# One core, eight blocks: the opening's loads, biases and masks are reordered, and three batches' expert rows are turned by VectorE and DMA

## The chip, the core and the metric

The kernel runs on one core of a Trainium2 chip. TensorE (PE) multiplies matrices, VectorE (DVE), ScalarE (ACT) and GpSimd (POOL) work on tiles, and SyncE (SP) starts transfers; ScalarE and GpSimd can start transfers too. The metric is the device time of one launch in microseconds (us).

## The reference

Four layers run over `x` (4 batches, 256 tokens, 256 features). Each adds a cross-attention over a context (4 batches, 512 rows of 128) and then a feed-forward block, both on the layer-normed `x`:

```python
...
    x = x + _L0_xattn_ref(_layernorm(x, axis=-1), ctx_1024, L0_xattn_Wq, ...)
    x = x + _L0_ffn_ref(_layernorm(x, axis=-1), L0_ffn_A, L0_ffn_B, L0_ffn_W, L0_ffn_bias)
    x = x + _L1_xattn_ref(_layernorm(x, axis=-1), ctx_1024, mask_BxS2_bf1, L1_xattn_Wq, ...)
...
```

Layer 0's attention has 16 heads of 16 lanes; queries and keys get a bias and are normed by head, and the last 16 rows of the context go through weights of their own (`Wkv_dca`, `bkv_dca`). Layer 0's feed-forward block takes, of 64 small experts (16 rows of A each), the four with the largest response to a token and adds their outputs to a dense product. The other layers' attention has 16 heads of 128; their blocks are gated experts, two experts by argmax, and a top-64 selection of tokens. Only layer 0 is touched by the change.

## The kernel before

`bounded_path` (L837) is the program that runs. In each engine's queue the order of the work is the order in which the Python code calls it, since the section is a hand-ordered schedule (L1055); transfers go to the queue of the engine that is named.

**The opening** (L1059 to L1596). SP loads x of batch 0 and the query weights `wq0`, then three short bias rows into `rows1` (its part `crow`: q's bias, the keys' bias, the bias of the special keys), then the second context, the second x, and the rest. ScalarE's queue loads the first context (`load_c(0)`, L872) and the weights `wkv` for keys and values. GpSimd loads the norms' parameters `prm`. A load uses one of eight transfer semaphores in turn, so with eight under way the next one waits for an earlier one.

TensorE begins with `warm(9)` (L1464): multiplications of the identity by itself, which have no use but to keep the engine busy. `context_T(0)` (L907) turns the four 128x128 blocks of the first context (pcT), and ScalarE copies them to `cT`. `Norm` (L915) takes mean and variance on DVE and the inverse root on GpSimd; `tokens` writes the normed rows; `layernorm_T` (L939) turns them by four TensorE blocks (pxn) and one copy by ScalarE. `centred` (L1178) takes each head's mean out of the weights and of the bias rows, on DVE. `rows_of_biases` (L1120) makes three rows of zeros and ones (`takes`), on GpSimd, that say which bias row a partition gets; `spread_biases` (L1188) multiplies them with `crow` (pbias), and ScalarE copies the result to `bqk`. `project_q` (L1207) multiplies queries (pq) and gives back the addition of the bias (DVE, L1219); `project_k` (L1223) does it for the keys (pk, L1235). Then squares, sums, powers and scales (class `Scale`) lead to the turned heads (pT) and to the first scores (ps L1401) at 20.96 us.

**Layer 0's attention** (L1707 to L1724). For each batch b and each of eight steps i (four groups of heads, two halves of the keys) the queues get, in this order: the scores of the step (16 products, in four of the six PSUM banks of one ring) and their exponentials on ScalarE (L1405); `ahead`; the products with the values of the group before (po); at odd steps `quotient` (L1428, DVE); and `between(b, i)` (L1613), which spreads the other work over the steps: the next batch's projections, norms and turned heads, the output of the batch before (`output0`), and at the end the beginning of the expert block.

`turned_aside` and `layernorm_aside` (L969) are another way to turn a tile: DVE turns blocks of 32x32 into `y`, and 16 transfers on SP's queue put the blocks in place. The contexts of batches 2 and 3 go this way.

**The expert block** (class `Arrows`, L1471; loop at L1749). Eight chunks of 128 tokens. `vectors` multiplies by `wa` (paf), `routes` picks four experts on DVE and ends with a product on GpSimd (L1514), `turned` turns that by TensorE (puT), `output` adds up (pyf). The normed rows `xnTs["f", k]` of batch k are turned by `layernorm_T`: batch 0 and 1 at steps 3 and 5 of the last batch's attention (L1698), 2 and 3 in the loop (L1767).

Of the kernel before, what the change touches and what calls it, by code (L numbers as in the profile page):

```python
# [836 lines left out]
def bounded_path(ctx: ExitStack, tc: tile.TileContext, t, out: bass.AP, over):  # L837
# [34 lines left out]
    def load_c(b):  # L872
        (nc.sync if b else nc.scalar).dma_start(c_sb[:, b], t["ctx"][b].rearrange("(k p) c -> p k c", p=P))
# [181 lines left out]
    with tc.manual_schedule(engines={E.PE, E.Activation, E.DVE, E.Pool}):  # L1055
# [4 lines left out]
        load_c(0)  # L1060
# [3 lines left out]
        wkv = l0.tile([P, 2, 2 * D], F32, tag="wkv", name="wkv")  # L1064
        nc.scalar.dma_start(wkv[:, 0, :], t["L0_wkv"])
# [5 lines left out]
        def by_head(w, x=HD0):  # L1071
            return w.rearrange("p n (h x) -> p n h x", x=x)


        rows1 = w0.tile([3, D + 3 * P], F32, tag="oT0", name="rows1")
        crow = rows1[:, :D].rearrange("n (o d) -> n o d", o=1)
        takes = rows1[:, D:].rearrange("n (i p) -> n i p", p=P)


        brow = l0.tile([1, 2, 2 * D], F32, tag="brow", name="brow")  # L1080
        nc.sync.dma_start(crow[0:1, 0, :], t["L0_bq"].partition_broadcast(1))
        for i, n in enumerate(("L0_bkv", "L0_bdca")):
            nc.sync.dma_start(
                crow[1 + i : 2 + i, 0, :].rearrange("o (h x) -> o h x", x=HD0),
                t[n].rearrange("(o h x) -> o h x", o=1, x=2 * HD0)[:, :, :HD0],
            )
# [101 lines left out]
        def spread_biases():  # L1188
            pb = bank("mm", [P, 2, D], "pbias0")
            for i in range(2):  # L1190
                nc.tensor.matmul(pb[:, i, :], lhsT=takes[:, i, :], rhs=crow[:, 0, :], start=True, stop=True)
            pl = bank("mm", [P, D], "pbias1")
            nc.tensor.matmul(pl, lhsT=takes[:, 2, :], rhs=crow[:, 0, :], start=True, stop=True)
            nc.scalar.copy(bqk[:, 0:2, :], pb)
            nc.scalar.copy(bqk[:, 2, :], pl)
# [111 lines left out]
        def columns_of_norms():  # L1307
            wide = [P, 3, 2, HD0]
            by_lane = l0.tile(wide, F32, tag="by_lane", name="by_lane")
            pairs = l0.tile([P, 3, 2], F32, tag="pairs", name="pairs")  # L1310
            nc.vector.tensor_tensor(by_lane, prm, lane0[:, 0, None, None, :].to_broadcast(wide), ALU.mult)
            nc.vector.tensor_reduce(pairs, by_lane, AX.X, ALU.add)
            for o in range(2):
                nc.vector.tensor_scalar(
                    cols[:, o, :], pairs[:, 0, :], halves0[:, o : o + 1], HD0 ** -0.5, ALU.mult, ALU.mult
                )
            nc.vector.tensor_copy(cols[:, 2:, :], pairs[:, 1:, :])
# [294 lines left out]

        def between(b, i):  # L1613

            n = b + 1
            if n == 1:
# [76 lines left out]
            if b == B - 1:  # L1693
                if i in (0, 2, 6):
                    norms["f", i // 2] = Norm(min(i // 2, 2), f"f0_{min(i // 2, 2)}")
                if i in (1, 3, 7):
                    xns["f", i // 2] = norms["f", i // 2].tokens()
                if i in (3, 5):  # L1698
                    k = (i - 3) // 2
                    xnTs["f", k] = layernorm_T(xns["f", k], f"f0_{k}")  # L1700
                if i == 4:
                    arrows[0] = Arrows(0)
                    arrows[0].vectors()
                if i == 5:
                    arrows[0].routes()
# [43 lines left out]
        for n in range(B * NC):  # L1749
# [1730 lines left out]
```

## Time and profile before

| what | us |
|---|---|
| median of 3 runs | 1381.64 (1380.35 to 1382.58) |
| the profiled execution | 1380.97 |
| its span | 1379.2 |
| first scores of layer 0 (ps L1401) | 20.96 |
| last products of layer 0's attention end | 137.4 |
| first query product of layer 1 (pq L1900) | 220.46 |

The span runs from the first to the last recorded instruction; the rest of the execution's time lies around it. A line of a timeline gives start, length, engine, line of the code, operation, output and inputs with their sizes, and in brackets the idle time before it with what ended it. Lines of the same kind that follow one another are merged (x4). PEld are the loads of TensorE's weights, which run beside its products. A letter q after an engine's name means its queue of transfers. A multiplication in float32 is recorded as two passes, so four products are x8, while turned blocks (pcT, pxn, pT) are recorded once each.

### The profile page before, as it was taken

Reading aid. Unit: us, or ns where it says so; the run is one execution under the profiler, and the core shown is the slowest. Engines: PE = TensorE matmul, PEld = TensorE weight load, DVE = VectorE, ACT = ScalarE, POOL = GpSimd, SP = SyncE. Lnnn points to the kernel's source line nnn. Section 1 sums busy time; section 2 is a strip of 40 time slices with the busy share of each in tenths; the row PEclk is TensorE's granted clock in tenths of the full one; section 3 lists DMA queues with packets and bytes.
Section 4 is the critical chain, followed back from the end, with each engine's and each line's share of the span. In section 5 each row is a group of like instructions: output and inputs, shape, how many; then the busy total and the mean of one; then the engine's idle time right before and its main releaser. Section 6 shows DMA issues by size and latency. Waiting matters only on the chain.

```text
span 1379.2 us, 20227 instructions
## 1 busy us (share of the span) xinstructions
PE 1369.2 (99%) x7221; PEld 903.1 (65%) x7221; DVE 897.2 (65%) x2052; ACT 572.6 (42%) x1134; POOL 699.4 (51%) x848
## 2 busy tenths in 40 slices
PE   9999999999999999999999999999999999999997
PEld 7665676566656667887565666666975665666666
DVE  6767863666666557655676756558656758566675
ACT  5766454433343332256434333333364334333331
POOL 5223333566565445352577655566325676444660
PEclk9999999999999999999999999999999999999999
DMA  5000220300000001361120000000432000000001
GB/s 171 15 3 2 77 78 17 89 19 8 16 5 19 0 13 43 83 218 48 47 54 15 17 0 16 0 1 16 124 119 69 7 12 4 1 8 1 0 1 34
DMA packets 77907, 50.79 MB, mean 37 GB/s; under 512 B 40628, under 2 KB 72645, under 8 KB 77799
## 3 DMA queue, kind: packets, MB, share of 16 engines
q1 hardware_dynamic: 72262, 36.13, 9.6%
q0 software_dynamic: 4176, 12.24, 3.1%
q8 instruction: 59, 0.97, 0.3%
q10 hardware_dynamic: 1360, 1.05, 0.2%
q14 instruction: 50, 0.40, 0.1%
HBM read 38.78 MB, written 6.95 MB: 33 GB/s over the span
## 4 chain that ended last, share of the span: by engine, by line
PE 97%; POOL 2%; DVE 1%; issue 0%; ACT 0%; POOLq 0%; DVEq 0%
PE ps L1948 23%; PE po L1956 23%; PE paq L1918 6%; PE pao L1918 5%; PE pbq L1918 4%; PE pbo L1918 4%; PE ps L1401 3%; PE po L1411 2%; PE pyf L1535 2%; PE paf L1485 2%; PE pgu L2496 2%; PE pm L1014 2%; PE psh L2317 2%; PE py L2042 2%; PE pn L1030 1%; PE pb L2901 1%
## 5 line engine op out<-in xcount | busy, mean ns | idle before, releaser
L1967 POOL TENSOR_TENSOR half<-pT 128x1024 f32<-128x1024 f32 x93 | 218.4, 2349 | 282.8 <-ACT pT L1951 228.0
L1948 PE MATMUL ps<-qT,cT 128*128 128x512 f32 x768 | 345.6, 593 | 0.0
L1956 PE MATMUL po<-pT,c_sb 128*128 128x512 f32 x768 | 345.3, 592 | 0.0
L1951 ACT ACTIVATE pT<-ps,mbias 128x512 f32<-128x512 f32 x384 | 263.8, 687 | 164.0 <-PE ps L1948 147.3
L1956 PEld LDWEIGHTS po<-pT,c_sb 128*128 128x128 f32 x768 | 145.8, 190 | 183.2 <-issue 183.2
L1948 PEld LDWEIGHTS ps<-qT,cT 128*128 128x128 f32 x768 | 138.9, 190 | 138.4 <-issue 136.1
L1960 ACT COPY oT<-po 128x512 f32<-128x512 f32 x96 | 56.2, 586 | 265.2 <-PE po L1956 265.2
L2003 POOL TENSOR_TENSOR oT<-oT,wide 128x512 f32<-128x512 f32 x84 | 106.8, 1291 | 0.0
L1928 DVE TENSOR_TENSOR qT<-qT,paq 128x128 f32<-128x128 f32 x90 | 25.2, 280 | 87.1 <-ACT qT L1927 87.1
L1405 ACT ACTIVATE pT<-ps 128x512 f32<-128x512 f32 x128 | 66.0, 602 | 21.6 <-PE ps L1401 21.4
L1975 DVE TENSOR_TENSOR half<-half 128x512 f32<-128x512 f32 x96 | 71.9, 749 | 2.7 <-POOL half L1965 2.5
L1977 DVE STREAM_TRANSPOSE turned<-half 128x512 f32<-128x512 f32 x96 | 68.3, 711 | 6.3
L1918 PE MATMUL paq<-xnT_a,m_sb 128*128 128x128 f32 x360 | 71.3, 280 | 0.0
L1928 DVE TENSOR_TENSOR w<-w,pao 128x128 f32<-128x128 f32 x21 | 6.0, 285 | 99.2 <-ACT w L1927 99.2
L1918 PE MATMUL paq<-xx,m_x 128*128 128x128 f32 x360 | 69.6, 275 | 0.0
L1918 PEld LDWEIGHTS paq<-xnT_a,m_sb 128*128 128x128 f32 x360 | 57.5, 192 | 18.2 <-issue 9.2
L1981 DVE TENSOR_REDUCE sums<-turned 128x16 f32<-128x512 f32 x96 | 65.9, 686 | 3.3
L1918 PE MATMUL pao<-n_x,ox 128*128 128x128 f32 x336 | 65.0, 275 | 0.0
L1927 ACT COPY qT<-paq 128x128 f32<-128x128 f32 x90 | 23.9, 265 | 94.2 <-PE paq L1918 93.2
L1931 DVE TENSOR_TENSOR qT<-qT,pbq 128x384 f32<-128x384 f32 x90 | 49.8, 554 | 9.4
L1918 PEld LDWEIGHTS paq<-xx,m_x 128*128 128x128 f32 x360 | 54.7, 192 | 0.0
L2002 DVE STREAM_TRANSPOSE wide<-rz 128x512 f32<-128x512 f32 x84 | 54.4, 686 | 0.0
(504 smaller groups left out, 2553.9 us busy)
## 6 DMA issues: line engine op xcount, KB each, us to landing
wq<-in_L_wqT SPq DMA_DIRECT2D x8, 512.0 KB
wo<-in_L_wo SPq DMA_DIRECT2D x8, 512.0 KB
yd<-yr SPq DMA_DIRECT2D x20, 128.0 KB
xnT_a<-y_a SPq DMA_DIRECT2D x144, 16.0 KB
xd<-xn_f SPq DMA_DIRECT2D x8, 256.0 KB
w<-in_F_w SPq DMA_DIRECT2D x4, 512.0 KB
wq<-in_L_wqT POOLq DMA_DIRECT2D x3, 512.0 KB
wo<-in_L_wo POOLq DMA_DIRECT2D x3, 512.0 KB
```

The source lines that it names most:

```text
L1405: nc.scalar.activation(pT[kp][:, j], ps[j], AF.Exp)
L1918: nc.tensor.matmul(p[:, at, :], lhsT=lhsT, rhs=rhs, start=(k == 0 and at == 0), stop=(k == len(of) - 1 and i == which[-1]),)
L1948: nc.tensor.matmul(ps, lhsT=cT[:, b, k * P : (k + 1) * P], rhs=qT, start=True, stop=True)
L1951: nc.scalar.activation(pT[:, k, :], ps, AF.Exp, bias=mbias[:, b, k : k + 1])
L1956: nc.tensor.matmul(po, lhsT=c_sb[:, b, k, :], rhs=pT[:, k], start=(k == 0), stop=(k == NK - 1))
L1960: done["head"] = nc.scalar.copy(raw, po).ins
L1967: nc.gpsimd.tensor_tensor(half, pT[:, 0:2], pT[:, 2:4], ALU.add)
L1975: nc.vector.tensor_tensor(part, half[:, 0], half[:, 1], ALU.add)
L1977: nc.vector.transpose(turned.rearrange("p f i -> p (f i)"), part)
L1981: nc.vector.tensor_reduce(sums[b, hp // 4][:, hp % 4, :], turned, AX.X, ALU.add)
L2002: nc.vector.transpose(wide, rzs[b, hp // 4][:, hp % 4, :, None].to_broadcast([P, NB, 32]))
L2003: eng.tensor_tensor(outs[b, hp], outs[b, hp], wide.rearrange("p f i -> p (f i)"), ALU.mult)
```

## The change

The three bias rows move to the front of ScalarE's queue of transfers, ahead of the first context, which is now called for after `wq0`. The masks `takes` are made by four copies of columns of the identity on DVE instead of memset and selects on GpSimd. `c_last` is zeroed after the first norm. The first context is turned behind the normed rows, the biases are centred ahead of `wq0` and spread ahead of the queries' products, one `warm(3)` before the rows' turning and one before the queries are gone, and the first warm-up has 11 products. In the expert block the rows of batch 0 are normed at step 2 and turned at step 3 of batch 2's attention, those of batch 1 at steps 0 and 1, and those of batch 2 at steps 6 and 7 of batch 3's attention, all three by DVE and 16 transfers each (`rows_of_arrows`) into tiles of their own (`xf`); those of batch 3 stay with TensorE. `kept` in `columns_of_norms` and the pair of calls of `spread_biases` change nothing in the order of what they hold.

```diff
@@ -1057,33 +1057,31 @@
         l0 = c0.enter_context(tc.tile_pool(name="l0", bufs=1, side="right"))
 
         load_x(0)
-        load_c(0)
-        wq0 = l0.tile([P, ND, D], F32, tag="wq0", name="wq0")
-        nc.sync.dma_start(wq0, t["L0_wq"].rearrange("(d p) n -> p d n", p=P))
-
-        wkv = l0.tile([P, 2, 2 * D], F32, tag="wkv", name="wkv")
-        nc.scalar.dma_start(wkv[:, 0, :], t["L0_wkv"])
-        nc.scalar.dma_start(wkv[:, 1, :], t["L0_wdca"])
-
-        prm = l0.tile([P, 3, 2, HD0], F32, tag="prm", name="prm")
-        nc.scalar.preload_act_table_set("natural_log_exp_and_others")
-
-        def by_head(w, x=HD0):
-            return w.rearrange("p n (h x) -> p n h x", x=x)
-
-
         rows1 = w0.tile([3, D + 3 * P], F32, tag="oT0", name="rows1")
         crow = rows1[:, :D].rearrange("n (o d) -> n o d", o=1)
         takes = rows1[:, D:].rearrange("n (i p) -> n i p", p=P)
-
-
-        brow = l0.tile([1, 2, 2 * D], F32, tag="brow", name="brow")
-        nc.sync.dma_start(crow[0:1, 0, :], t["L0_bq"].partition_broadcast(1))
+        nc.scalar.dma_start(crow[0:1, 0, :], t["L0_bq"].partition_broadcast(1))
         for i, n in enumerate(("L0_bkv", "L0_bdca")):
-            nc.sync.dma_start(
+            nc.scalar.dma_start(
                 crow[1 + i : 2 + i, 0, :].rearrange("o (h x) -> o h x", x=HD0),
                 t[n].rearrange("(o h x) -> o h x", o=1, x=2 * HD0)[:, :, :HD0],
             )
+        wq0 = l0.tile([P, ND, D], F32, tag="wq0", name="wq0")
+        nc.sync.dma_start(wq0, t["L0_wq"].rearrange("(d p) n -> p d n", p=P))
+
+        wkv = l0.tile([P, 2, 2 * D], F32, tag="wkv", name="wkv")
+        load_c(0)
+        nc.scalar.dma_start(wkv[:, 0, :], t["L0_wkv"])
+        nc.scalar.dma_start(wkv[:, 1, :], t["L0_wdca"])
+
+        prm = l0.tile([P, 3, 2, HD0], F32, tag="prm", name="prm")
+        nc.scalar.preload_act_table_set("natural_log_exp_and_others")
+
+        def by_head(w, x=HD0):
+            return w.rearrange("p n (h x) -> p n h x", x=x)
+
+
+        brow = l0.tile([1, 2, 2 * D], F32, tag="brow", name="brow")
         load_c(1)
         load_x(1)
         for i, n in enumerate(("L0_bkv", "L0_bdca")):
@@ -1118,17 +1116,11 @@
         pad = l0.tile([P, NQK, 2, P], F32, tag="pad", name="pad")
 
         def rows_of_biases():
-            nc.gpsimd.memset(takes, 1.0)
-            for i, base, cm, p in (
-                (0, 0, -1, 0), (1, -1, 1, 0), (1, 1, -1, 0), (2, RD - 1 - P, P, -1), (2, 2 * P - RD, -P, 1),
-            ):
-                nc.gpsimd.affine_select(
-                    out=takes[:, i, :], in_=takes[:, i, :], compare_op=ALU.is_ge, fill=0.0, base=base,
-                    pattern=[[p, P]], channel_multiplier=cm,
-                )
+            for i, n, h in ((0, 0, slice(0, P)), (1, 1, slice(0, P)), (2, 1, slice(0, RD)), (2, 2, slice(RD, P))):
+                w = takes[:, i, h]
+                nc.vector.tensor_copy(w, ident[:3, n : n + 1].to_broadcast([3, h.stop - h.start]))
 
         c_last = l0.tile([P, 2, 2, P], F32, tag="c_last", name="c_last")
-        nc.gpsimd.memset(c_last, 0.0)
         lane0 = l0.tile([P, 2, HD0], F32, tag="lane0", name="lane0")
         halves0 = l0.tile([P, 2], F32, tag="halves0", name="halves0")
         nc.vector.tensor_reduce(
@@ -1185,14 +1177,11 @@
 
         bqk = l0.tile([P, 3, D], F32, tag="bqk", name="bqk")
 
-        def spread_biases():
-            pb = bank("mm", [P, 2, D], "pbias0")
-            for i in range(2):
-                nc.tensor.matmul(pb[:, i, :], lhsT=takes[:, i, :], rhs=crow[:, 0, :], start=True, stop=True)
-            pl = bank("mm", [P, D], "pbias1")
-            nc.tensor.matmul(pl, lhsT=takes[:, 2, :], rhs=crow[:, 0, :], start=True, stop=True)
-            nc.scalar.copy(bqk[:, 0:2, :], pb)
-            nc.scalar.copy(bqk[:, 2, :], pl)
+        def spread_biases(a, z):
+            pb = bank("mm", [P, z - a, D], f"pbias{a}")
+            for i in range(a, z):
+                nc.tensor.matmul(pb[:, i - a, :], lhsT=takes[:, i, :], rhs=crow[:, 0, :], start=True, stop=True)
+            return lambda: nc.scalar.copy(bqk[:, a:z, :], pb)
 
         qks, xnTs = {}, {}
 
@@ -1310,11 +1299,15 @@
             pairs = l0.tile([P, 3, 2], F32, tag="pairs", name="pairs")
             nc.vector.tensor_tensor(by_lane, prm, lane0[:, 0, None, None, :].to_broadcast(wide), ALU.mult)
             nc.vector.tensor_reduce(pairs, by_lane, AX.X, ALU.add)
-            for o in range(2):
-                nc.vector.tensor_scalar(
-                    cols[:, o, :], pairs[:, 0, :], halves0[:, o : o + 1], HD0 ** -0.5, ALU.mult, ALU.mult
-                )
-            nc.vector.tensor_copy(cols[:, 2:, :], pairs[:, 1:, :])
+
+            def kept():
+                for o in range(2):
+                    nc.vector.tensor_scalar(
+                        cols[:, o, :], pairs[:, 0, :], halves0[:, o : o + 1], HD0 ** -0.5, ALU.mult, ALU.mult
+                    )
+                nc.vector.tensor_copy(cols[:, 2:, :], pairs[:, 1:, :])
+
+            return kept
 
         def score_bound():
 
@@ -1538,28 +1531,27 @@
                 nc.gpsimd.tensor_tensor(x_sb[b][:, c, :], x_sb[b][:, c, :], ys, ALU.add)
 
 
-        warm(9)
-        context_T(0)
+        warm(11)
+        rows_of_biases()
         norm = Norm(0, "a0_0")
-        rows_of_biases()
-        last_context(0)
+        nc.gpsimd.memset(c_last, 0.0)
         mq = head_sums(by_head(wq0))
         xn = norm.tokens()
-        warm(3)
+        centred(by_head(crow), by_head(crow), head_sums(by_head(crow), 3), 3)
         xnTs[0] = layernorm_T(xn, "a0_0")
+        context_T(0)
+        last_context(0)
+        for a, z in ((0, 2), (2, 3)):
+            spread_biases(a, z)()
         centred(by_head(wq0), by_head(wq0), mq)
-        centred(by_head(crow), by_head(crow), head_sums(by_head(crow), 3), 3)
         wk = by_head(wkv, 2 * HD0)[:, :, :, :HD0]
         centred(by_head(wk0), wk, head_sums(wk))
         for n in range(2):
             wv = by_head(wkv, 2 * HD0)[:, n, :, HD0:].rearrange("p (q j o) x -> p o q j x", q=2, o=2)
             for o in range(2):
                 nc.gpsimd.tensor_copy(wvo[:, n, o].rearrange("p (q j) x -> p q j x", q=2), wv[:, o])
-        columns_of_norms()
-        warm(3)
-        add_q = project_q(0)
-        spread_biases()
-        add_q()
+        columns_of_norms()()
+        project_q(0)()
         sc0 = Scale(0)
         sc0.square(True, 0, NC)
         add_k = [project_k(0, k0) for k0 in range(0, NK, 2)]
@@ -1610,9 +1602,18 @@
                 elif i == 7 and n > 1:
                     transposed(n, 4)
 
+        def rows_of_arrows(k):
+            xnT = early.tile([P, ND, S], F32, tag="xf", name=f"xnT_f0_{k}", bufs=3)
+            xnTs["f", k] = layernorm_aside(norms["f"].tokens(), f"f0_{k}", xnT, True)
+
         def between(b, i):
 
             n = b + 1
+            if b == B - 2:
+                if i == 2:
+                    norms["f"] = Norm(0, "f0_0")
+                elif i == 3:
+                    rows_of_arrows(0)
             if n == 1:
                 if i == 0:
                     for k0 in range(0, NK, 2):
@@ -1691,13 +1692,10 @@
                     for j in range(1, 4):
                         nc.vector.tensor_copy(quad[:, 32 * j : 32 * (j + 1)], quad[:, :32])
             if b == B - 1:
-                if i in (0, 2, 6):
-                    norms["f", i // 2] = Norm(min(i // 2, 2), f"f0_{min(i // 2, 2)}")
-                if i in (1, 3, 7):
-                    xns["f", i // 2] = norms["f", i // 2].tokens()
-                if i in (3, 5):
-                    k = (i - 3) // 2
-                    xnTs["f", k] = layernorm_T(xns["f", k], f"f0_{k}")
+                if i in (0, 6):
+                    norms["f"] = Norm(1 + i // 6, f"f0_{1 + i // 6}")
+                if i in (1, 7):
+                    rows_of_arrows(1 + i // 6)
                 if i == 4:
                     arrows[0] = Arrows(0)
                     arrows[0].vectors()
@@ -1762,9 +1760,8 @@
                 if n:
                     arrows[n].output()
             else:
-                k = n // NC + 2
-                if k < B:
-                    xnTs["f", k] = layernorm_T(xns["f", k + (k == 2)], f"f0_{k}")
+                if n == 3:
+                    xnTs["f", 3] = layernorm_T(xns["f", 3], "f0_3")
                 if n == 7:
                     first_xnT = layernorm_T(xn1, "a1_0")
                     next(fold)
```

More of the change, by code (lines that the diff above doesn't have):

```diff
@@ L1059, in bounded_path @@
         load_x(0)
-        load_c(0)
+        rows1 = w0.tile([3, D + 3 * P], F32, tag="oT0", name="rows1")
+        crow = rows1[:, :D].rearrange("n (o d) -> n o d", o=1)
+        takes = rows1[:, D:].rearrange("n (i p) -> n i p", p=P)
+        nc.scalar.dma_start(crow[0:1, 0, :], t["L0_bq"].partition_broadcast(1))
+        for i, n in enumerate(("L0_bkv", "L0_bdca")):
+            nc.scalar.dma_start(
+                crow[1 + i : 2 + i, 0, :].rearrange("o (h x) -> o h x", x=HD0),
+                t[n].rearrange("(o h x) -> o h x", o=1, x=2 * HD0)[:, :, :HD0],
+            )
         wq0 = l0.tile([P, ND, D], F32, tag="wq0", name="wq0")
@@ L1072, in by_head @@
             return w.rearrange("p n (h x) -> p n h x", x=x)
-        rows1 = w0.tile([3, D + 3 * P], F32, tag="oT0", name="rows1")
-        crow = rows1[:, :D].rearrange("n (o d) -> n o d", o=1)
-        takes = rows1[:, D:].rearrange("n (i p) -> n i p", p=P)
         brow = l0.tile([1, 2, 2 * D], F32, tag="brow", name="brow")
-        nc.sync.dma_start(crow[0:1, 0, :], t["L0_bq"].partition_broadcast(1))
-        for i, n in enumerate(("L0_bkv", "L0_bdca")):
-            nc.sync.dma_start(
-                crow[1 + i : 2 + i, 0, :].rearrange("o (h x) -> o h x", x=HD0),
-                t[n].rearrange("(o h x) -> o h x", o=1, x=2 * HD0)[:, :, :HD0],
-            )
         load_c(1)
@@ L1312, in columns_of_norms @@
             nc.vector.tensor_reduce(pairs, by_lane, AX.X, ALU.add)
[L1313 to L1317 removed]
+            def kept():
+                for o in range(2):
+                    nc.vector.tensor_scalar(
+                        cols[:, o, :], pairs[:, 0, :], halves0[:, o : o + 1], HD0 ** -0.5, ALU.mult, ALU.mult
+                    )
+                nc.vector.tensor_copy(cols[:, 2:, :], pairs[:, 1:, :])
+            return kept
         def score_bound():
```

## The prediction

> **What bounds the kernel now.** I read the page first, then the chain of waits for the first 26 us, the timeline of the three places that the change touches (0 to 26, 90 to 138, 138 to 220 us), SP's waits, and the tile views of the turned rows. The page's first part:
>
> ```profile
> PE 1369.2 (99%) x7221; PEld 903.1 (65%) x7221; DVE 897.2 (65%) x2052; ACT 572.6 (42%) x1134; POOL 699.4 (51%) x848
> ```
>
> TensorE is the bound nearly everywhere: work taken off it counts in full, work put on DVE counts only where TensorE then waits. The opening is the exception, since part of its busy TensorE is filler (pwarm). The chain of waits, 0 to 26 us (start, length, what):
>
> ```profile
> 5.74 0.85 PE pcT L911 x4
> 6.59 1.10 PE pwarm L1468 x6
> 7.69 0.44 PE pxn_a L945 x4
> 8.12 0.67 PE pwarm L1468 x6
> 8.79 0.01 issue
> 8.80 1.99 PE pq L1212 x8
> 10.79 1.06 PE pbias L1191 x4
> 11.85 0.43 PE pbias L1193 x2
> 12.28 1.07 PE pk L1229 x4
> 13.36 0.02 issue
> 13.38 0.69 DVE qk L1235
> ```
>
> The reader is to see that TensorE's queue carries the chain up to the first keys (end of pk, 13.36), and that from 13.38 DVE carries it to 17.7. The timeline shows beside it when data come, and SP's waits when the loads land:
>
> ```profile
> 8.71 0.41 DVE L1175 TENSOR_REDUCE hm<-rows 3x16 f32<-3x256 f32 x1 [0.98 <-DMA rows<-in_L_bdca]
> 12.50 0.69 DVE L1219 TENSOR_TENSOR qk<-pq,bqk 128x512 f32<-128x512 f32 x1 [0.56 <-ACT bqk L1194]
> SPq L873 <- DMA wkv<-in_L_wdca: 1.5, 1, 1.5
> SPq L873 <- DMA c_sb<-in_ctx: 1.3, 1, 1.3
> ```
>
> The bias rows arrive at 8.71. The addition of q's bias waits for them until 12.50, but it ends at 13.19, before pk's 13.36: it costs the chain almost nothing.
>
> **The change, part 1: the opening.** Removed from TensorE's path: two warm(3), 1.10 + 0.67 = 1.77 us. Two more warm-ups (4 records of some 0.21, 0.85 in all) fill the place of the four turned blocks of the first context (pcT), so the filler again ends at 6.59. pcT now stands behind pxn. The bias products are only put ahead of pq; TensorE's sum to the end of pk holds them either way. So this reordering removes no time from the chain, only q's wait, which was not last.
>
> New sum: pxn needs the normalised rows (DVE L933, 6.21 + 0.83 = 7.04), so with two blocks before and two after it ends at 7.45. Then pcT 0.44 (pxn's own four blocks, now warm), pbias 1.06 + 0.43, pq 1.99, pk 1.07: 4.99 us. If pcT starts at T, pk ends at T + 4.99, and the gain is 13.36 - 4.99 - T = 8.37 - T. With T = 7.45 that is 0.92 us.
>
> T hangs on the first context's landing. Its issue stood on ScalarE's queue at 0.81 and landed when SP's waiting L873 went on, at 4.75. Now three bias rows stand ahead of it; their issues took 0.37, 0.66 and 0.60 on SP, so it is issued at 2.44. SP, freed of the rows, issues c1 and x1 right behind wq (1.72 and 2.14, not 4.75 and 5.21, as only six to eight loads are out then). So four loads of 256 KB (x0, wq, c1, x1) are issued ahead of the context, where it was second. In the trace the fourth such load, wkv, landed at 6.16 (SP's L1090 goes on) and the fifth, wdca, at 8.20 (L873): bandwidth falls from some 350 to mostly below 60 GB/s between about 6.4 and 7.2 us, while the three rows loaded by POOL are on the same engines. T lies between 7.45 (like wkv) and 8.25 (like wdca); I take 8.17, near the fifth, which it is. Gain 0.2 us, bounds 0.9 and, a further 1 us late, -0.8.
>
> Here a rule speaks against the change. The Trainium skill, "DMA: Bandwidth & Descriptors", section "Issuing engines are not separate DMA queues", says that loads started by different engines run on the same 16 engines and interleave; another queue saves only issue time. The row agrees in part: c_sb and x_sb were issued at 0.81 and 0.80, and the context landed 0.8 us later. With a queue of its own the context would land 3.94 us after its issue as before, at 6.4, and the gain be 0.92; by the rule it is pushed back by c1 and x1, and the gain is 0.2. I follow the rule.
>
> The rest: the four mask copies on DVE (0.16 each by L1317, 0.25 by L1692: 0.6 to 1.0 us) lie in DVE's wait for x (2.31 to 3.92); without it they would cost that. POOL loses its five selects and a memset; c_last's memset (0.56) moves behind rstd and is done before the context is turned. The bias rows' own sums (0.41 + 0.42) now run at 7.04 to 7.87, and put wq's centring from 6.96 to 7.87 to 8.64; pq starts at 10.1, so it is hidden. wkv and wdca are sixth and seventh or later; I estimate 9.5 from the fifth's 8.20 and 0.73 us per load at 350 GB/s. Keys' weights are then ready at 9.5 + 0.67 + 0.78 = 10.95, before pk (12.1); the norms' columns (1.05) end at 12.0, where q's addition wants to start. Another 0.5 us late would be hidden, more counts one for one. ACT's table load (1.28) moves to about 4 and is done before its first copy at 7.5.
>
> Clock: the profile's granted clock reads 1.00 throughout, yet 128x128 blocks take 0.21 each until 7.3 and 0.11 after. The Trainium skill, "TensorE: Matmul & The Clock Gate", Part 1, says half rate lasts until a window of some 3.4 us was busy, and returns after an idle one. The trace took 5.7 us from the first warm-up. By the row nothing changes (TensorE stays busy to 7.45, idles 0.7); by the rule a spoilt window would keep half rate to about 10.7: 1.2 us lost. I take 0, and keep 1.2 for the range.
>
> **Part 2: expert rows of batches 0 to 2.** Removed: three groups of four turned blocks and three copies on ACT (0.585 each). Added: six DVE turns and 48 DMAs on SP.
>
> ```profile
> L945 PE MATMUL pxn_f<-ident,xn_f x16: 272/273/327, 119.2 to 175.5; 128*128 128x128 f32 x16
> L973 DVE STREAM_TRANSPOSE y_f<-xn_f x6: 401/420/439, 346.4 to 509.3; 128x256 f32<-128x256 f32 x6
> 95.70 1.74 DVE L1276 TENSOR_REDUCE hv<-hs 128x96 f32<-128x1536 f32 x1
> 98.60 0.30 ACT L1282 ACTIVATE hr<-hv 128x96 f32<-128x96 f32 x1
> 104.27 1.77 PE L1401 MATMUL ps<-qT,kT 32*128 32x256 f32 x16
> 150.59 1.93 POOL L1514 TENSOR_TENSOR twof<-routef,vf 128x1024 f32<-128x1024 f32 x1 [3.82 <-DVE vf L1513]
> 154.90 1.04 PE L1522 MATMUL puTf<-ident,twof 128*128 128x128 f32 x8
> ```
>
> TensorE: 0.66 + 0.60 + 0.60 = 1.86 us (119.2, 129.9, 155.8), all on its back-to-back queue. ACT's 1.75 us and the copies' waits for buffers go too, off the path.
>
> DVE, batch 0's rows: Norm(0) (1.4 us) falls into an idle stretch (87.2 to 90.7). The rows and two turns (1.14, as in the rows beside a busy POOL, + 0.84 = 1.98) stand behind the quotient that ends at 95.78 and ahead of hv, which starts at 97.8, not 95.70. Queued behind hv's sum: ACT's hr, 98.60 to about 99.7, and behind that all eight exponentials of the next two steps, which free the score banks, then qT, whose end lets ps at 104.27 finish (1.77 for the usual 1.15: it already waits for ACT). Cost 0 to 1.1 us; I take 0.9. Batch 1's rows add 0.84 at 117.7, where two Norms' 1.4 and 0.7 leave DVE soon after: nothing. Batch 2's turns (0.84) push DVE's unbroken run to 150.4, so twof ends at 152.52 + 0.84; puTf at 154.90 comes 0.60 earlier relative to that run: slack 2.38 falls to 0.94, and for the next arrow 2.88 to 0.84. Nothing, but gone if DVE slips 1 us more.
>
> SP: a set of 16 issues took 10.8 us for cT (59.90 on), and 1.3 us more to land: some 12 us. Batch 0's land by 110 (needed 122.9), batch 1's by 131 (140.9), batch 2's by 155 (about 158.5). SP's next loads (layer 1's weights, 153.72) are at most 1 us later, needed at 168. Net of part 2: 1.86 - 0.9 = 1.0 us.
>
> **Sum.** 0.2 + 1.0 = 1.2 us. The profiled execution: 1380.97 with a span of 1379.2; it becomes 1379.8 with 1378.0. The median is 0.67 above that execution: 1381.64 - 1.2 = 1380.4.
>
> **Rivals.** *All covered* (0.20): the context lands by 7.4, and batch 0's turns hide: 0.92 + 1.86 = 2.8, with x's earlier landing up to 3.2: 1378.7. For it: TensorE's share of 99%; against it: the bandwidth gap at 6.4 us. *Late context* (0.20): the loads pushed behind c1 and x1 land past 9.2, where 8.37 - T eats part 2's 1.0; at T = 10 the end is 0.8 later (1382.4), with half rate 2.0 (1383.6). Slower from T = 9.2 on. For it: wdca's 6.34 us from issue to landing; against: only four loads stand ahead. *It does not reach the end* (0.10): the second layer waits for something fixed and 0 remains, 1381.6; against: TensorE is busy for 198.7 of the 199 us from 21 to 220. Forecast 0.50 (1379.4 to 1381.3).
>
> A difference below 0.2% (2.76 us) can hardly be told from none here. Faster by more: over half of *all covered* and a little of the forecast, 0.14; slower: the tail of *late context*, 0.08; within: 0.78. Range 1378.3 to 1383.2.
>
> **What would show it.** First row of pcT after 7.9 and no DMA gain for it: right; at 7.5: *all covered*; after 9.2: *late context*. First keys' addition (L1235) at 13.2; half-rate blocks after 8 us would show the clock. ACT hr in batch 2 at 99.7 less the opening's gain, and ps near 104 stretched; if they have not moved, my 0.9 is wrong. No L945 rows at 119, 130 and 156. If TensorE waits for xnT_f at about 158, SP's chain was mis-sized.

## The result and the profile after

| | before | after |
|---|---|---|
| median of 8 runs each | 1381.79 (1380.27 to 1383.65) | 1385.45 (1383.26 to 1386.09) |
| ratio, 95% interval | | 1.0025 [1.0014, 1.0036]: slower |
| the profiled execution, its span | 1380.97, 1379.2 | 1383.37, 1381.7 |
| first scores of layer 0 | 20.96 | 25.73 |
| first sums of layer 1 (pz), at 264.3 before | | 3.75 later |
| last TensorE product | | 4.22 later |
| from VectorE's last instruction to the end of the span | 6.2 | 4.5 |

The change is 3.7 us slower; 1380.4 was forecast, 1378.3 to 1383.2 the range. The row that carries most of it stands in the chain of waits of the changed kernel, 0 to 26 us (start, length, what):

```profile
2.72 7.21 DMA c_sb<-in_ctx
9.92 0.04 issue
9.97 0.66 PE pcT L911 x4
10.62 1.88 PE pbias L1183 x6
12.50 3.71 PE pq L1201 x8
16.21 2.88 PE pk L1218 x8
```

The first context is a link of the chain now: issued at 2.72, there at 9.92, so T, the start of pcT, is 9.97. And pq takes 3.71 where the same eight records took 1.99. VectorE's rows give the end of that stretch:

```profile
6.99 0.41 DVE L1167 TENSOR_REDUCE hm<-rows 3x16 f32<-3x256 f32 x1 [0.28 <-DMA rows<-in_L_bdca]
...
11.38 0.69 DVE L1167 TENSOR_REDUCE hm<-wkv 128x32 f32<-128x512 f32 x1 [2.94 <-DMA wkv<-in_L_wdca]
...
16.32 0.69 DVE L1208 TENSOR_TENSOR qk<-pq,bqk 128x512 f32<-128x512 f32 x1 [2.19 <-PE pq L1201]
17.96 0.69 DVE L1224 TENSOR_TENSOR qk<-pk,bqk 128x512 f32<-128x512 f32 x1 [0.95 <-PE pk L1218]
```

The bias rows do come 1.7 us earlier (6.99 for 8.71), as the change wants, but the first keys' addition starts at 17.96 and not at 13.38. The busy times by stretch (window; then busy us of PE, PEld, DVE, ACT, POOL; granted clock, share of the transfer engines, GB/s) show both causes side by side. Before:

```profile
4.00:6.00 2.00, 2.00 (x12) 2.00 (x11) 1.60 (x6) 0.00 (x0) 0.55 (x1) 1.00 1.22 352
6.00:8.00 2.00, 2.00 (x14) 2.00 (x13) 1.73 (x4) 0.59 (x1) 2.00 (x7) 1.00 0.84 150
```

and after:

```profile
4.00:6.00 2.00, 1.78 (x13) 1.59 (x11) 1.61 (x6) 0.91 (x1) 1.02 (x3) 1.00 0.63 105
6.00:8.00 2.00, 0.75 (x4) 0.40 (x4) 1.69 (x5) 0.96 (x2) 0.25 (x1) 1.00 0.93 184
8.00:10.00 2.00, 0.03 (x1) 0.03 (x1) 0.45 (x1) 0.00 (x0) 0.00 (x0) 1.00 1.01 356
10.00:12.00 2.00, 2.00 (x10) 1.49 (x10) 0.62 (x1) 0.87 (x2) 0.60 (x4) 0.90 1.00 320
12.00:14.00 2.00, 2.00 (x6) 1.30 (x5) 1.90 (x7) 0.68 (x2) 1.93 (x9) 0.50 0.97 285
```

From 4 to 6 us only 105 GB/s move (352 before, where a dip to 150 came from 6 to 8, behind the context's landing at 4.75): that is when the context should come. TensorE is all but idle from 7.2 to 9.97. Its granted clock is still 1.00 while it waits, and 0.50 after, from 11.6 to 18.4.

**Where the 4.22 us of TensorE come from.** Its rows can be laid on those of before, product by product. The lag is 4.77 at the first scores and stays there to 100 us (opening); becomes 5.43, then 5.10 at 106 (batch 0's rows on VectorE); falls to 4.44 at 121, 4.00 at 131, 3.75 at 164 (the three groups of turned blocks that are gone). So part 2 gives 1.02. Behind 264 us another 0.47 is lost, most of it in layer 1's gated experts; I have no cause for it. The end of the span gives 1.76 back, so the span is 2.46 longer (1381.65 against 1379.19).

The single executions of the changed kernel differ by up to 2.8 us, and their mean granted clock goes with it: the two changed executions near 1383.3 have 0.997, the six others, 1385.2 to 1386.1, have 0.994 to 0.996; of before, those at 1380 to 1381 have mostly 0.998 or 0.999, those above 1383 have 0.996. The profiled execution of after is one of its quickest: it is 2.4 slower than the one of before, the medians differ by 3.7. The remaining 1.3 is in executions that were not profiled; their lower mean clock speaks for more half rate there, and where it lies is open.

### The profile page after: what moved, and what is told of

Same layout as the page of the kernel before. It is cut to its first block, busy times and chain, and to the rows that moved or that the text cites. A ratio compares the mean times of both kernels' runs of the same rounds, so it can differ in the third digit from the quotient of the medians.

```text
span 1381.7 us, 20260 instructions
## 1 busy us (share of the span) xinstructions
PE 1369.7 (99%) x7201; PEld 902.1 (65%) x7201; DVE 901.0 (65%) x2062; ACT 571.5 (41%) x1131; POOL 697.5 (50%) x842
## 3 DMA queue, kind: packets, MB, share of 16 engines
q10 hardware_dynamic: 1426, 1.05, 0.2%
## 4 chain that ended last, share of the span: by engine, by line
PE 95%; POOL 2%; DMA 1%; issue 1%; DVE 1%; ACTq 0%; ACT 0%; POOLq 0%; DVEq 0%
PE ps L1945 23%; PE po L1953 23%; PE paq L1915 6%; PE pao L1915 5%; PE pbq L1915 4%; PE pbo L1915 4%; PE ps L1394 3%; PE po L1404 2%; PE pyf L1528 2%; PE paf L1478 2%; PE psh L2314 2%; PE py L2039 2%; PE pgu L2493 1%; PE pm L1014 1%; PE pn L1030 1%; PE pb L2898 1%
```

## The experiments

Theory A: the context's late landing and the half rate behind it are the whole loss. Rivals: the new order of TensorE loses the clock in any case; part 2 costs. All numbers come from one profile each (most of the opening repeats to within some tenths of a us; with the same loads, after, kept_warm and opening_alone have pcT at 9.97, 10.29 and 10.72, so a landing is known to 0.8 only), times from the runs beside runs of before. Half rate: how long the granted clock was 0.50, in the opening and again near 570 us. TensorE at 264: its lag on the rows of before (minus: ahead). End: from VectorE's last instruction to the end of the span.

| kernel | pcT | first scores | half rate in the opening, us | near 570, us | TensorE at 264 | end | time, ratio to before |
|---|---|---|---|---|---|---|---|
| before | 5.53 | 20.96 | 0 | 0 | 0 | 6.2 | 1381.79 |
| after | 9.97 | 25.73 | 6.83 | 0 | +3.75 | 4.5 | 1385.45, 1.0025 [1.0014, 1.0036] |
| part2_alone | 5.53 | 21.07 | 0 | 0 | -0.91 | 4.5 | 1378.26, 0.9979 [0.9970, 0.9988] |
| opening_alone | 10.72 | 26.59 | 6.83 | 6.83 | +5.63 | 6.4 | 1388.88, 1.0049 [1.0034, 1.0064] |
| part2_earlier | 5.53 | 20.98 | 0 | 3.41 | -1.05 | 4.5 | 1377.79, 0.9973 [0.9962, 0.9984] |
| context_first | 7.53 | 22.26 | 3.41 | 3.41 | +0.29 | 4.5 | 1381.17, 0.9998 [0.9990, 1.0007] |
| kept_warm | 10.29 | 22.92 | 0 | 3.41 | +0.95 | 4.5 | 1382.16, 1.0009 [1.0002, 1.0016] |
| loads_before | 7.72 | 22.99 | 3.41 | 0 | +1.01 | 4.5 | 1382.28, 1.0004 [0.9996, 1.0012] |
| first_and_warm | 7.12 | 21.41 | 0 | 3.41 | -0.57 | 4.6 | 1378.80, 0.9984 [0.9975, 0.9993] |
| rows_whole | 10.58 | 26.45 | 6.83 | 3.41 | +4.47 | 4.5 | 1385.20, one execution |
| seconds_behind | 9.78 | 25.55 | 6.83 | 0 | +3.57 | 4.4 | 1382.72, one execution |
| prm_behind | 8.57 | 24.44 | 6.83 | 0 | +2.47 | 4.4 | 1382.51, one execution |
| prm_by_sync | 10.40 | 26.86 | 10.24 | 3.41 | +4.89 | 4.5 | 1385.40, one execution |
| prm_spread | 8.22 | 24.32 | 6.83 | 3.41 | +2.35 | 4.7 | 1382.14, 1.0001 [0.9992, 1.0010] |
| all_three | 7.36 | 24.51 | 3.41 | 0 | +2.46 | 4.6 | 1381.55, 1.0001 [0.9992, 1.0010] |
| spread_and_first | 7.56 | 21.30 | 0 | 3.41 | -0.72 | 4.6 | 1379.98, 0.9987 [0.9978, 0.9996] |
| spread_no_filler | 7.60 | 20.45 | 0 | 6.83 | -1.59 | 4.7 | 1379.47, 0.9985 [0.9976, 0.9994] |
| before_more_issues | 5.54 | 20.70 | 0 | 3.41 | +7.29 | 4.9 | 1386.24, 1.0027 [1.0017, 1.0037] |

### Which part loses

**part2_alone**: the kernel before with the second part only (`rows_of_arrows` and its three calls).

> The kernel before with the expert rows of batches 0 to 2 turned by VectorE, and its opening untouched. Theory (the loss of the change lies wholly in the opening; part 2 is worth what the prediction said): first scores at 20.96 as before, last TensorE product about 1.0 earlier, time ratio to before 0.9993 (1.0 us less). Rival (part 2 brings nothing, or costs through VectorE or SP): ratio 1.000 or above, with ps of the next batch or twof later by as much as TensorE saves.

TensorE gains 1.03 between the first scores and 264, by the same steps as in the changed kernel. But the profiled execution is 2.9 quicker (1378.10 for 1380.97), as the end of the span is 1.7 shorter as well, and the median 3.5.

**opening_alone**: the changed kernel with the second part undone.

> The changed kernel with the expert rows of batches 0 to 2 turned by TensorE as before: the opening of the change alone. Theory (the two parts add up, and the whole loss is the opening's): first scores at 25.7, all of TensorE's work up to 264 us later by 4.8 than before with no step at 101 and none between 118 and 164; time some 1 us above the changed kernel. Rival (the parts act on each other): a step of over 0.2 us between 30 and 264. Aside: the kernel before ends 6.2 us behind its last VectorE instruction, all changed ones so far 4.5; if that belongs to the second part, this kernel shows 6.2.

No step between 31 and 264: the lag is 5.63 throughout. The parts add up, and the opening carries the whole loss. At the first scores it lost 0.9 more than in the changed kernel, with the context 0.75 later. The end is 6.4: the short end belongs to part 2. By the medians part 2 is worth 3.4 here (1388.88 against 1385.45), where 1 was expected.

**part2_earlier**: part 2 alone, batch 0's norm and rows one step earlier.

```diff
-                if i == 2:
+                if i == 1:
                     norms["f"] = Norm(0, "f0_0")
-                elif i == 3:
+                elif i == 2:
                     rows_of_arrows(0)
```

> Part 2 alone (opening as before), with batch 0's norm at step 1 and its rows and turns at step 2 of batch 2's attention, where VectorE stands idle for 2.26 us until 90.8, and not at steps 2 and 3. Theory (the step of 0.66 at 101 us comes from the turns ahead of hv): no step at 101, TensorE 1.3 to 1.7 ahead of the kernel before at 264 in place of 0.9. Rival (the delay comes from elsewhere, SyncE's sets of 16 or the norm): the step stays.

The step at 101 is gone, but one of 0.27 stands at 86.6 (time of before) in its place; over the whole part 2 gives 1.07 and not 1.03, less than was expected. The delay goes with the place of the turns; the idle time that I wanted to fill was needed too.

### The landing or the clock

**context_first**: the changed kernel with `load_c(0)` ahead of the bias rows on ScalarE's queue.

> The changed kernel with the first context back at the head of ScalarE's queue, the three bias rows right behind it. Theory (the late context holds TensorE, and the wait costs the clock): the context lands by about 5, pcT follows pxn at about 7.2 and not at 9.97; what then comes last are the bias rows (pieces that were slow to land in both kernels, 7 to 9): first scores between 20.5 and 22.5, time 2.5 to 4.5 us below the changed kernel. Rival (TensorE's new order without the warm-ups loses the clock however early the context is): pcT early, but half-rate rows between 10 and 18 all the same and first scores past 24.

pcT follows pxn at once, and first scores come at 22.26, inside what theory A said. But half rate came all the same, from 9.8 to 13.2, as the rival had it, though half as long. TensorE's timeline (start, length; idle before in brackets):

```profile
8.66 1.82 PE L1183 MATMUL pbias<-rows 3*128 3x256 f32 x6 [0.52 <-DVE rows L1172]
10.40 3.37 PE L1201 MATMUL pq<-wq,xnT_a 128*128 128x256 f32 x8
```

No other stop of TensorE lies between 5.5 us and this stretch than a gap of 0.38 ahead of pxn and the one of 0.52 here.

**kept_warm**: the changed kernel with filler in TensorE's long gap.

```diff
         xnTs[0] = layernorm_T(xn, "a0_0")
+        warm(11)
         context_T(0)
```

> The changed kernel with eleven warm-ups (22 records) between the turned rows and the turned context, where TensorE stood idle for 2.76 us; loads untouched. Theory: the context still lands at about 9.9, so pcT still starts at about 10.0, but the clock stays at 1.00 from 11.6 to 18.3, pq takes 1.99 and not 3.7, first scores at about 22.7 (3.0 earlier than the changed kernel's 25.75), time 3 us below it. Rival (half rate has another cause than the wait): granted clock 0.5 from 11.6 on as before, first scores past 25.

```profile
7.27 2.62 PE L1461 MATMUL pwarm<-ident 128*128 128x128 f32 x22
10.29 0.66 PE L911 MATMUL pcT<-ident,c_sb 128*128 128x128 f32 x4 [0.39 <-DMA c_sb<-in_ctx]
10.87 1.56 PE L1183 MATMUL pbias<-rows 3*128 3x256 f32 x6
12.36 1.99 PE L1201 MATMUL pq<-wq,xnT_a 128*128 128x256 f32 x8
15.26 0.69 DVE L1224 TENSOR_TENSOR qk<-pk,bqk 128x512 f32<-128x512 f32 x1
```

The context lands even later, pq takes 1.99 again, and first scores come 2.8 earlier. The first keys' addition starts at 15.26; the prediction's sum, T + 4.99, gives 15.28. So with the clock kept the sum of the prediction holds to 0.02, and half rate alone costs 17.96 - (9.97 + 4.99) = 3.0 us in the changed kernel.

**loads_before**: all loads as before, the rest as changed.

> The changed kernel with all loads in the order and on the queues of the kernel before (context first on ScalarE's, rows on SyncE's behind wq0, ahead of c1 and x1); masks, order of TensorE and part 2 as changed. Theory: context at 4.75, bias rows at 8.7, their two sums end at 9.5, the bias products wait for them: TensorE idle for some 2 us between 7.5 and 9.6, pk ends at about 14.1 (0.7 later than before) if the clock stays, 2 to 3 later if a wait of this length costs it too. Rival (it is the order of the loads alone): first scores at 21 or earlier.

The bias products wait for the rows (sums start at 8.44, pbias at 9.35), then 3.41 us of half rate: first scores 2.0 later than before. So the new order of TensorE is no gain with the old loads, as it has the bias products wait for rows that the old order needed only later.

**first_and_warm**: context first, and filler in the two gaps.

```diff
-        warm(11)
+        warm(12)
...
         context_T(0)
+        warm(3)
         last_context(0)
```

> The kernel with the context first on ScalarE's queue (the second experiment) with twelve warm-ups in place of eleven at the start and three more between the turned context and the bias products, so that TensorE has no gap of 0.4 and 0.5 us there. Theory (any gap in the opening can cost a stretch of half rate of some 3.4 us, however short it is): clock 1.00 from 8 us on, pq 1.99 and not 3.37, first scores at 20.6 (1.7 earlier than without the warm-ups), time at the level of part 2 alone, 1378 us. Rival (the gaps are too short to matter and the stretch of half rate came from the early part): half rate again between 9.8 and 13.3, first scores at 22.3.

Clock 1.00 throughout, pq 1.99, but the rows came at 8.54 this time and TensorE stood 1.05 us idle for them: 21.41, not 20.6. That this gap cost no half rate contradicts my "any gap".

### What makes the context late

Three suspects: the pieces of the bias rows ahead of it on ScalarE's queue, the 512 KB of c1 and x1, GpSimd's loads of the norms' parameters `prm`. With the loads as changed pcT starts between 9.97 and 10.72 (three kernels); a smaller move than that says little.

**rows_whole**: the keys' bias rows in one piece each.

```diff
-                crow[1 + i : 2 + i, 0, :].rearrange("o (h x) -> o h x", x=HD0),
-                t[n].rearrange("(o h x) -> o h x", o=1, x=2 * HD0)[:, :, :HD0],
+                crow[1 + i : 2 + i, 0, :], t[n][:D].partition_broadcast(1),
```

> The changed kernel with the two rows of the keys' biases loaded as one piece of 256 numbers each in place of 16 pieces of 16 (other numbers of the same vectors, so the keys' biases are not the reference's). Everything else as changed. If the pieces in front of the context on ScalarE's queue are what holds it back: the context lands at 6 to 8 and pcT starts before 8.5. If it is the share of the transfer engines that c1 and x1 take, or the parameters loaded by GpSimd: pcT stays at 9.5 to 10.3.

pcT at 10.58, within that spread: not the pieces.

**seconds_behind**: c1 and x1 issued by ScalarE behind `wdca`.

> The changed kernel with the second context and the second x called for by ScalarE behind the weights of keys and values, not by SyncE right behind wq0. If these two (512 KB ahead of the first context) are what holds it back: context lands about 1.5 earlier, pcT at 8.0 to 8.6. If it is the pieces of the bias rows, or GpSimd's loads: pcT stays at 9.5 to 10.3.

pcT at 9.78, with 512 KB less in front, is 0.2 below the lowest of the three and 0.9 below the highest; 1.5 was expected. It was by counting such loads that the prediction came to its T. The rate from 4 to 6 us is still low, 83 GB/s; what these 512 KB would weigh without the dip was not tried.

**prm_behind**: the three loads of `prm` behind the first inverse root.

> The changed kernel with the three loads of the norms' parameters on GpSimd's queue issued behind the inverse root of the first norm (after 5.8 in place of 1.6). If the packets of these loads stall the transfer engines between 4 and 8 us: the rate between 4 and 6 us stays near 380 GB/s, context at about 7.5, pcT before 8.5. If not: pcT stays at 9.5 to 10.3.

pcT at 8.57, the largest move of the three, though the rate from 4 to 6 us is 244 and not near 380. The rate (last column):

```profile
4.00:6.00 2.00, 2.00 (x12) 2.00 (x11) 1.59 (x6) 1.01 (x1) 0.73 (x2) 1.00 0.91 244
6.00:8.00 2.00, 1.29 (x7) 0.70 (x6) 1.96 (x5) 0.86 (x2) 1.99 (x4) 1.00 1.01 347
8.00:10.00 2.00, 1.43 (x7) 1.19 (x8) 0.19 (x2) 0.59 (x1) 0.35 (x2) 0.93 0.86 270
10.00:12.00 2.00, 2.00 (x5) 1.15 (x4) 1.38 (x2) 0.96 (x2) 1.93 (x8) 0.50 0.86 176
```

A dip stands at 10 to 12 now. The packets of these three loads are under way from 8.25 to 11.98 here (3.81 to 8.62 in the changed kernel), and the rate is lowest, 100 GB/s, from 10 to 11.

**prm_by_sync**: the same loads by SyncE, behind `wq0`.

> The changed kernel with the three loads of the norms' parameters on SyncE's queue behind wq0, issued at about the same time as GpSimd issued them. If it is GpSimd's queue (its descriptors) that makes the transfer engines stand idle from 4 to 6 us: the rate there stays above 200 GB/s and the context lands by about 8.5, as with the loads issued late. If it is what they read (one row of 128 bytes, 128 times over): the dip stays, pcT at 9.5 or later.

```profile
4.00:6.00 2.00, 1.84 (x13) 1.65 (x11) 1.58 (x7) 1.28 (x1) 0.83 (x2) 1.00 0.38 73
```

The dip stays, deeper than in the changed kernel: it isn't GpSimd's queue. The Trainium skill, "SBUF: two separate sides" in "SBUF — State Buffer", tells of loads from GpSimd's queue that stall for want of descriptors while VectorE runs an instruction in a two-port mode, and of another engine's queue as the remedy; no run here shows that stall, and here the remedy brings no gain.

**prm_spread**: the parameters read once, into one partition, and spread by a product.

```diff
-            nc.gpsimd.dma_start(prm[:, i], t[f"L0_{n}"].partition_broadcast(P))
+            nc.gpsimd.dma_start(prow[0:1, 2 * HD0 * i : 2 * HD0 * (i + 1)], t[f"L0_{n}"].partition_broadcast(1))
...
         context_T(0)
+        nc.tensor.matmul(pp, lhsT=takes[:, 0, :], rhs=prow, start=True, stop=True)
+        nc.scalar.copy(prm.rearrange("p i j x -> p (i j x)"), pp)
```

> The changed kernel with the norms' parameters loaded into one partition (three pieces of 128 bytes, on GpSimd's queue as before) and spread to all by a product with the first mask and a copy by ScalarE; nothing reads one row 128 times. Theory (these reads alone cause the dip): rate above 250 GB/s from 2.5 to 7 us, context at 7.0 to 8.3, pcT before 8.4, first scores 1.5 to 2 earlier than the changed kernel's 25.75 (half rate still there, if the gap costs it). Rival (the 32 pieces of the bias rows hold the context back too): a dip stays between 4 and 6 us, pcT after 9.

```profile
4.00:6.00 2.00, 2.00 (x13) 2.00 (x11) 1.64 (x7) 0.90 (x1) 1.11 (x4) 1.00 0.89 239
6.00:8.00 2.00, 0.98 (x7) 0.44 (x5) 1.97 (x5) 0.97 (x2) 0.29 (x1) 1.00 0.98 337
8.22 0.66 PE L911 MATMUL pcT<-ident,c_sb 128*128 128x128 f32 x4 [0.98 <-DMA c_sb<-in_ctx]
```

239 GB/s (250 were expected) and pcT at 8.22: freed of these reads the context lands where the prediction had it. So 1.75 of the late landing are theirs (2.5 against the latest of the three kernels): three loads that fetch one row of 128 bytes for each of 128 partitions. In the changed kernel the trace has 48 packets of 1 KB for them, which take 0.44 us each in the mean and up to 1.35, where other packets of 1 KB in the first 16 us take 0.05. Whether it is the same address or the small pieces was not tried. The half rate stays, 6.83 us behind gaps of 0.26 and 0.98, so the first scores come 1.4 earlier, a little less than expected.

### The other end, and a better opening

**before_more_issues**: the kernel before, SyncE with 46 instructions more.

```diff
-... lambda w: [(w, t["F0_wT"].rearrange("(d p) n -> p d n", p=P))] ...
+... lambda w: [(w[8 * i : 8 * i + 8, d], t["F0_wT"][d * P + 8 * i : d * P + 8 * i + 8]) for d in range(ND) for i in range(P // 8)] ...
```

(and `F0_bT` likewise, in 16 pieces)

> The kernel before with the loads of two weights of the expert block cut up into 32 and 16 pieces, so that SyncE has 46 instructions more (part 2 adds 48), all of them early and needed late. Theory (the end's length hangs on where SyncE's last instructions lie in its program): the stretch from the last VectorE instruction's end to the end of the span falls from 6.2 to 4.5, nothing else moves, time 1.5 to 1.9 below before. Rival (the shorter end comes from something else in part 2): 6.2 as before, time unchanged.

The end falls to 4.9, not quite to 4.5. As a test of time it failed: a context comes late, TensorE stands 4.8 us until 55.84, and its clock is 0.50 from 54.6 to 61.4; together they cost 7.5. SyncE's waits in the last stretch (who, for whom: total, times, longest), of before:

```profile
SPq L3412 <- SPq L3412: 2.8, 1, 2.8
```

and of after:

```profile
SPq L3409 <- SPq L3409: 1.0, 3, 0.5
```

In before_more_issues it is 1.4, in opening_alone 2.9. So the standstill of SyncE behind its last store is long in the two kernels without the 46 or 48 more instructions, and short with them. What SyncE waits for the profile doesn't name, so why the number of its instructions should matter stays open.

**all_three**: context first, filler, `prm` behind, batch 0's rows earlier.

> The changed kernel with what the runs so far point to: context first on ScalarE's queue and the bias rows behind it, twelve and three warm-ups, the norms' parameters loaded by GpSimd behind the first inverse root, batch 0's rows at step 2 of batch 2. Theory (the reads of the norms' parameters make the transfers slow, wherever they stand; warm-ups keep the clock): rate above 200 GB/s from 2.5 to 7 us, rows there by 7.5, bias products at 8 and not at 9.45, clock 1.00 throughout, first scores at 20.2 to 20.7, time 0.3 to 0.8 us below part 2 alone: 1377.4 to 1378. Rival (the parameters then come too late: the columns that VectorE makes of them stand ahead of q's addition): q's addition waits for them past 12.5, first scores at 21.5 or later, and nothing is won on part 2 alone.

The rival was right: pk starts at 11.87, but the parameters land at 13.8, VectorE waits 3.65 for them, first scores at 24.51.

**spread_and_first**: `prm_spread` with context first and filler.

> The same spreading, with the context first on ScalarE's queue, the bias rows behind it, twelve and three warm-ups, batch 0's rows at step 2 of batch 2. Theory: rows there by 7.4, parameters long before VectorE's 10.2, so q's addition starts at 12.0 and the first keys' at 13.0 (13.38 before), first scores at 20.4 to 20.7, clock 1.00; TensorE 1.3 to 1.6 ahead of before at 264, time 0.3 to 0.6 below part 2 alone. Rival (rows or parameters still come late): first scores past 21, nothing won on part 2 alone.

21.30: rows at 7.61, but now my own filler lasts to 9.3 while the rows' sums are done at 8.44.

**spread_no_filler**: the same without `warm(3)`.

> The previous best opening (parameters spread by a product, context first) without its three warm-ups ahead of the bias products, which TensorE was still at when the bias rows were ready (8.44). Theory: bias products at 8.5 and not 9.34, first scores at 20.5 and not 21.3, TensorE 1.5 ahead of before at 264, time about 0.5 below part 2 alone, 1377.6. Rival (without the filler the clock is lost again): half rate for 3.4 or 6.8 us, first scores past 22.

```profile
8.43 1.48 PE L1185 MATMUL pbias<-rows 3*128 3x256 f32 x6
9.84 1.99 PE L1203 MATMUL pq<-wq,xnT_a 128*128 128x256 f32 x8
```

First scores at 20.45, 0.5 earlier than before, and TensorE 1.59 ahead at 264: the best opening of all. Its time, 1379.47, is no better than that of part 2 alone: the profiled execution loses 3.0 between 540 and 690 us by 6.83 us of half rate from 567.3 on. part2_earlier has the lowest median here (1377.79), but the intervals of its ratio, of part2_alone's and of this kernel's overlap.

## Why the prediction was wrong, point by point

- **"T lies between 7.45 and 8.25; I take 8.17": failed, 9.97.** The rule that another queue saves only issue time sent me the right way, later than before, but I counted loads ahead of the context, and 512 KB less ahead moved it by 0.2 to 0.9 us, within what the landing scatters. I had seen the dip of the rate at 6.4 to 7.2 us and that POOL's rows were on the engines then, and I let it stand where it was. In the changed kernel the rate falls at 3.5 and is back only at 8. prm_spread shows what these reads cost: without them T = 8.22. That this lies so near to my 8.17 is in part luck, as I took that from a landing (8.20) which itself lay behind the dip of before.
- **"By the rule a spoilt window would keep half rate to about 10.7: 1.2 us lost. I take 0": failed, 3.0.** I asked only when TensorE would reach the full clock; I didn't ask what a gap does once it has it. With T = 9.97 my own "idles 0.7" became 2.76. The clock fell at 11.6, when TensorE had been back at work for 1.6 us, and the bias products' end, pq and the keys ran at half rate.
- Why the number failed, in one sum. The opening: 8.37 - 9.97 = -1.6, less 3.0 for the clock is -4.6; measured 13.38 - 17.96 = -4.58, and 4.77 at the first scores. The formula was right, and these two terms of it were mis-sized: the landing by 1.8, the clock by 3.0.
- **Part 2, net 1.0: right, by two errors.** The three groups gave 0.66 + 0.44 + 0.25 = 1.35 for the 1.86 of their durations; batch 0's rows cost 0.33 for 0.9. VectorE's rows in batch 2 (timeline):

```profile
100.40 1.14 DVE L933 TENSOR_SCALAR xn_f<-x_sb,mv_f,rstd_f 128x256 f32<-128x256 f32 x2
101.46 0.76 DVE L973 STREAM_TRANSPOSE y_f<-xn_f 128x256 f32<-128x256 f32 x2
102.14 1.70 DVE L1265 TENSOR_REDUCE hv<-hs 128x96 f32<-128x1536 f32 x1
```

  hv stands behind the rows as predicted; ScalarE's hr starts at 104.13, which less 4.78 is 99.35, 0.75 later than before and not 1.1. The products behind it lose 0.66 and regain 0.33. The only turned rows left are batch 3's, and TensorE doesn't wait for xnT_f at 158: SP's chain was well sized.
- **The end of the span: no term at all**, and 1.7 us of gain. With it part 2 is worth 2.9 by the profiled executions, 3.4 to 3.5 by the medians, and not 1.0.
- Hidden as said: the masks (0.81 us, 2.23 to 3.04), c_last's memset, wdca late. wdca landed at 11.38 and not at 9.5 (by its own figures, 8.20 and twice 0.73, the estimate comes to 9.66), but pk started at 16.2.
- **The rivals.** *Late context* is what happened. Its sums were a little off: 8.37 - T eats 1.0 at T = 9.37 and not 9.2, and at T = 10 the loss is 0.63 and not 0.8. The rule itself held where the clock was kept: kept_warm, T = 10.29, is 0.95 behind at 264, where 8.37 - T + 1.0 gives 0.92. The price at T = 10 with half rate, 1383.6, is near the profiled execution's 1383.37 by luck: half rate cost 3.0 and not 1.2, and 1.7 came back at the end. I gave it 0.20 and let its tail end at 1383.2. The chance should have been larger: a landing that hangs on seven transfers, with a known dip that nothing pins to its place, is not known to 0.8 us.
- "The median is 0.67 above that execution": it is 2.1 above it. By their mean clock most other executions have one more stretch of half rate or more. Only one execution of this kernel was profiled, and in it there is none behind the opening; eleven other kernels show such stretches near 570.

## What to carry over

When loads are reordered, first ask what makes the rate dip, not how many bytes stand ahead, and suspect loads that fetch one row for every partition: spread them on the chip. When filler is taken out of a warm engine's queue, price the gap that opens with half rate for a window or two, above all where the gap's length hangs on a transfer. Compare executions by their granted clock and look at the end of the span, before a gain or loss of 2 us is put down to the edit.

## What the runs showed of the hardware

- Half rate comes in whole stretches: 3.41, 6.83 and 10.24 us in the openings of ten kernels. At half the clock 3.41 us hold 1.7 us of work, so up to 1.7 is lost by each. The length fits the window of some 3.4 us that the Trainium skill gives in "TensorE: Matmul & The Clock Gate", Part 1. The page asks for an idle window; before_more_issues fits that (4.8 us standing, and the clock falls within them). In the openings less was enough: in the ten kernels TensorE stood 0.90 (context_first) to 2.81 us (all_three) of the 3.41 us before the clock fell. Six kernels whose clock held had at most 0.70 in any 3.41 us from 5.5 us on, but first_and_warm held it with 1.05 and kept_warm with 1.08. So the idle time alone doesn't decide; where it lies in a window could, which was not tried.
- Half rate also comes near 570 us, where TensorE has no gap of note (0.03 us in the 3.41 before it): 0, 3.41 or 6.83 us in different kernels. It moves the time by as much as the change itself.
- The three loads of 16 KB that fetch one row for 128 partitions go with a rate of all transfers of 73 to 105 GB/s from 4 to 6 us, on GpSimd's queue (105) and on SyncE's (73) alike, where 239 move with the row read once.
- The end of the span is 1.7 us shorter in the kernels with 48 more instructions on SyncE, 1.3 with 46 more of another kind. The reason is open.
